# A resting rule for background chains, and a hand-laid start of the last attention

## The chip, the cores and the metric

The kernel runs on one core of one Trainium2 chip. Its time is the device time of one execution in microseconds (us), the median over several executions. All data are fp32. The core has a matrix engine (PE, with its weight loads shown apart as PEld), a vector engine (DVE), an activation engine (ACT), a general engine (POOL) and a sync engine (SP) that issues most of the DMAs. Each engine works through its own instructions strictly in the order in which the program lists them, and waits in place where an instruction's inputs are not there yet.

## The reference

Four layers, each an attention-like block and a feed-forward block, both with a residual connection and a layer norm before and after. x is 8 batches of 512 rows of 128 numbers.

```python
x = x + ln(attn0(ln(x)))     # softmax attention, 16 heads of 8; norm of its output over a whole batch
x = x + ln(mix(ln(x)))       # two mixes with the row before, sigmoid gate, squared relu
x = x + ln(learn(ln(x)))     # a scan: batch b's gradient step gives the weights for batch b and later ones
x = x + ln(switch(ln(x)))    # each row to one of 8 experts, half capacity, in order of rows
x = x + ln(linear_attn(ln(x)))
x = x + ln(experts(ln(x)))   # 8 experts choose 512 rows each, results are scatter-added
x = x + ln(rope_attn(ln(x))) # softmax attention with rotary positions, 16 heads of 8
x = x + ln(ffn4(ln(x)))      # 4 dense experts, 128 to 512 to 128, weighted per row

def ln(x):
    m = jnp.mean(x, axis=-1, keepdims=True)
    v = jnp.var(x, axis=-1, keepdims=True)
    return (x - m) / jnp.sqrt(v + 1e-5)
```

The scan in learn and the order of rows in switch make batches follow one another; everything else is independent from batch to batch up to the experts, which need all rows.

## The kernel before

A batch of x lies in SBUF as 128 partitions by 4 blocks (NJ = 4) by 128. The program is written with Python generators: there is no scheduler behind it, so the order in which the generators are advanced is the order of instructions on every engine.

**First attention.** `Attention.run` loops over g. There are 32 calls (8 batches, 4 groups of 4 heads), and a call has 4 values of g. In one g it issues 4 score matmuls (at_s, L410), each followed by a maximum on DVE (at_mx, L411), and, 7 values of g later for the same data, 4 transposed score matmuls (at_st, L417), each followed by an exponential on ACT (at_e, L420). Once in 4 values of g, `bg.rest()` runs, then the weighted sums of a whole call (at_o, 16 matmuls, L428), then `bg.pull`, then `taken`, which copies at_o out of PSUM on ACT (at_ot, L439). In the other three values of g only `bg.pull` runs. PSUM is used as a ring of 8 banks: score k+8 needs the bank of score k, so PE cannot run ahead of DVE and ACT by more than one g. With a bank for at_o the same holds.

**Background.** Beside the attention, `Background` advances generators ("chains"): `project` (norm, projections and stores for the next batch), `residuals`, `Mix.chain`, `Learn.prepare`, `Learn.chain`, `Learn.serve_chain` and `Route.chain`. A piece of a chain is what lies between two yields. Each yield gives an estimate of PE and DVE time, and `free(...)` marks a piece that may also be taken in `rest`. `pull` gives each chain one turn, until the estimates reach their bounds; `rest` makes two passes over the chains that are marked free, until the DVE estimate reaches 6. A gap below means what `rest` and the `pull` behind it do at one g, or a `pull` alone.

**A norm in a chain.** `norm_pieces` (L221) does: statistics on DVE (`stats`, L203 to L188) and the power on POOL (L194); yield free; a second yield free (`soft`, left out when `cx.brisk`); the offset on DVE (L211) and four scalings on ACT (L217); yield free; a `soft` yield. Up to three steps of a chain can thus fall into one gap with `rest`, so that the offset can stand on DVE right behind the power that it needs, and the scalings on ACT ahead of at_ot. `residuals` waits six turns after a batch's attention results were stored before it adds them.

**Rounds.** When the loop is over, `cx.brisk` is set and `Rounds.turn` advances what is left of the chains, and the new chains `Passes` (the switch layer's experts, in two passes: after 5 batches are routed and after 8) and `Pairs` (linear attention and the scores of the experts), one step each per round. Then `Experts.run` gathers, computes and scatter-adds (L1710).

**Last attention.** `l3` runs the same loop with `Background(3.3, 2.5)`, where `beside` is None and `rest` does nothing; the last layer's feed-forward is its background. Before the loop can start, `project(0)` must be done: `Experts.residual` loads four partial sums of batch 0 (L1749, four DMAs of 256 KB on SP), adds them (DVE for batch 0, POOL for others, L1754), norms the sum, adds it to x (POOL, L1758); then x is normed, turned (L239), copied (L240) and multiplied (L1790), and the rotary step goes over DVE and POOL (L1792 to L1801). `fill` (L376) then issues four loads of q and k (L381) and one of zeros (L382) on SP.

Of the kernel before, what the change touches and what calls it, by code (L numbers as in the profile page):

```python
# [17 lines left out]
P = 128  # L18
B = 8
S = 512  # L20
# [50 lines left out]
class Ctx:  # L71


    def __init__(self, es: ExitStack, tc: tile.TileContext, consts: bass.AP):
# [23 lines left out]
        self.brisk = False  # L98

# [121 lines left out]
    def norm_pieces(self, dst, src, last=0.0):  # L221

        mv, rs = self.stats(src)
        yield free(0.0, 1.5)
        yield from self.soft(free())
        self.affine(dst, src, rs, self.offset(mv, rs))
        yield free()
        yield from self.soft(last)
# [18 lines left out]

def costs(c):

    return (*c, False)[:3] if isinstance(c, tuple) else (c or 0.0, 0.0, False)  # L250


class Background:
# [14 lines left out]

    def add(self, gen):
        self.first.append(gen)  # L270
# [4 lines left out]
    def step(self, queue, gen):  # L275
        try:
            pe, dve, is_free = costs(next(gen))
        except StopIteration:
            queue.remove(gen)
            return  # L280
        self.pe += pe
        self.dve += dve
        (self.free.add if is_free else self.free.discard)(gen)

# [6 lines left out]
    def rest(self):  # L291

        if self.beside is None:
            return
        for _ in range(2):
            for gen in list(self.first):
                if self.dve >= self.beside:
                    return
                if gen in self.free:
                    self.turn(gen)  # L300
# [10 lines left out]
    def pull(self, spent=0.0):  # L311
# [4 lines left out]
        for gen in list(self.first):  # L316
            if self.pe >= max(pe - spent, 1.0) or self.dve >= dve:
                break
            self.turn(gen)
# [18 lines left out]
class Attention:  # L338
# [37 lines left out]
    def fill(self, n, sources, v):  # L376
# [3 lines left out]
        for h, src in enumerate(sources):  # L380
            nc.sync.dma_start(t[32 * h : 32 * h + 8], src)  # L381
# [104 lines left out]
def l0(cx: Ctx, at: Attention, Wq, Wk, Wv, mix, learn):  # L486
# [86 lines left out]
    def residuals():  # L573
        for b in range(B):
            while b not in finished:
                yield free()
            for _ in range(1 if cx.brisk else 6):
                yield free()
# [3 lines left out]
    def residual(b):  # L582
        y, xn = ys.pop(b), xns.pop(b)
        nc.gpsimd.tensor_add(y, y, xn)
        yield from cx.soft(free())
# [22 lines left out]
        yield free(0.2)  # L608
# [5 lines left out]
        yield free()  # L614
# [16 lines left out]
class Mix:  # L631
# [41 lines left out]
    def batch(self, b):  # L673
# [40 lines left out]
        yield free()  # L714


class Learn:
# [219 lines left out]
    def serve(self, b, xt, weights):  # L937
# [25 lines left out]
        yield free()  # L963
# [476 lines left out]
class Experts:  # L1440
# [303 lines left out]
    def residual(self, cx, b):  # L1744
# [7 lines left out]
        adds = nc.gpsimd if b else nc.vector  # L1752
        for i, k in ((0, 1), (2, 3), (0, 2)):
            adds.tensor_add(parts[:, i], parts[:, i], parts[:, k])  # L1754
# [14 lines left out]
def l3(cx: Ctx, at: Attention, experts, ffn, weights):  # L1769
# [8 lines left out]

    def project(b):
        yield from experts.residual(cx, b)  # L1780
        xn = cx.work([P, NJ, D], "xn")
        yield from cx.norm_pieces(xn, cx.x[b])
        xt = cx.work([P, S], "xnT")
        cx.flip(xt, xn)
        yield 0.5
# [196 lines left out]
def kernel(ctx: ExitStack, tc: tile.TileContext, a: dict, out: bass.AP):  # L1982
# [7 lines left out]
    with cx.phase("first"):  # L1990
# [6 lines left out]
        cx.brisk = True  # L1997
# [88 lines left out]
```

## Time and profile before

| what | value |
|---|---|
| three timed runs, us | 2119.72, 2121.99, 2127.91; median 2121.99 |
| profiled execution, its own time and its span, us | 2127.56 and 2125.8 |
| busy share of the span | PE 82%, DVE 60%, ACT 51%, POOL 24% |
| mean granted PE clock | 0.874 |
| first attention, first at_s to last at_o | 41.2 to 716.9 us |
| rounds, experts, to the last scatter L1710 | to 1299.8 us |
| start of the last attention, to its first at_s | to 1336.9 us |
| last attention and the end of the feed-forward | to 2125.8 us |

The span runs from the first to the last instruction; the profiled execution's own time is 1.8 us more. A sum of durations from the trace is compared with this execution, 5.6 us above the median of the timed runs. Busy PE counts matmuls in flight, so a PE that shows 95% is not at its peak.

### The profile page before, as it was taken

The page shows a single profiled execution, that of the slowest core. Times are in us where ns is not written, and L with a number is a line of the kernel's source. Part 1 is how long each engine was busy: PE and PEld are TensorE (multiplying, and loading weights), DVE is VectorE, ACT ScalarE, POOL GpSimd, SP SyncE. Part 2 cuts the span into 40 slices and gives each one's busy share as a digit, 9 for nine tenths or more (in the row PEclk, how much of TensorE's full clock was granted, in tenths as well). Part 3 has the DMA queues.
Part 4 walks back from the last instruction along what each step waited for, and adds up shares of the span by engine and source line. Part 5 has one row for each costly group of instructions (what it writes and reads, how often), then busy time and mean ns, then how long its engine had stood idle before and what let it go on. Part 6 is the DMA issues. An engine that isn't in the chain of part 4 may idle for free.

```text
span 2125.8 us, 31834 instructions
## 1 busy us (share of the span) xinstructions
PE 1740.0 (82%) x10886; PEld 1001.3 (47%) x10886; DVE 1282.0 (60%) x4012; ACT 1086.6 (51%) x2272; POOL 501.3 (24%) x566
## 2 busy tenths in 40 slices
PE   3999888988988777658546783799999999999996
PEld 1444344444434366547335562434554454545554
DVE  2777778767777546456447322777666666665522
ACT  1667656555554523256551221366666565565653
POOL 1001111212120312352523385222112121110001
PEclk8999899989999769569565786799999999999998
DMA  5212102111000213025223132111101010100000
GB/s 129 40 34 37 34 14 39 26 28 33 21 21 12 59 35 106 21 65 150 74 65 110 23 43 38 31 32 29 25 10 32 12 27 11 29 12 6 9 6 10
DMA packets 198065, 81.84 MB, mean 38 GB/s; under 512 B 97604, under 2 KB 189674, under 8 KB 197904
## 3 DMA queue, kind: packets, MB, share of 16 engines
q1 hardware_dynamic: 190224, 73.61, 14.4%
q0 software_dynamic: 7680, 6.19, 1.9%
q8 instruction: 87, 1.43, 0.3%
q14 instruction: 74, 0.61, 0.1%
HBM read 45.25 MB, written 31.59 MB: 36 GB/s over the span
## 4 chain that ended last, share of the span: by engine, by line
PE 31%; DVE 10%; POOL 4%; issue 3%; ACT 3%; DMA 1%; SPq 0%; POOLq 0%; ACTq 0%; DVEq 0%
PE at_s L410 6%; PE l3f_y_ps L1954 5%; PE at_o L428 5%; PE l3f_h_ps L1947 5%; DVE at_mx L411 4%; PE at_st L417 3%; POOL l2f_out L1710 2%; PE flip L239 1%; POOL l2f_xg L1105 1%; DVE ln_st L203 1%; PE l_qkv_ps L1790 1%; DVE l2f_junk L1530 1%; DMA l2f_xg<-l2f_x,l2f_idx 1%; DVE l_u L1799 1%; POOL ln_rs L194 1%
## 5 line engine op out<-in xcount | busy, mean ns | idle before, releaser
L411 DVE TENSOR_REDUCE at_mx<-at_s 128x1 f32<-128x512 f32 x1024 | 637.3, 682 | 287.2 <-PE at_st L417 219.6
L420 ACT ACTIVATE at_e<-at_st 128x512 f32<-128x512 f32 x1024 | 536.6, 600 | 197.4 <-PE at_st L417 170.7
L410 PE MATMUL at_s<-qk 32*128 32x512 f32 x2048 | 591.5, 655 | 44.6 <-DMA qk<-qk_zero 20.7
L417 PE MATMUL at_st<-qk 32*128 32x512 f32 x2048 | 582.5, 644 | 8.8 <-ACT at_ot L439 5.5
L410 PEld LDWEIGHTS at_s<-qk 32*128 32x128 f32 x2048 | 229.1, 194 | 196.0 <-DVE at_mx L411 62.8
L194 POOL TENSOR_TENSOR ln_rs<-ln_ve,mhalf 128x4 f32<-128x4 f32 x136 | 138.4, 1018 | 767.8 <-DVE ln_ve L188 701.7
L428 PE MATMUL at_o<-at_e,pad_v 128*32 128x512 f32 x2048 | 252.2, 636 | 35.4 <-DVE at_mx L411 35.4
L417 PEld LDWEIGHTS at_st<-qk 32*128 32x128 f32 x2048 | 229.7, 189 | 84.4 <-issue 47.0
L428 PEld LDWEIGHTS at_o<-at_e,pad_v 128*32 128x32 f32 x2048 | 67.2, 116 | 213.0 <-issue 178.8
L1954 PEld LDWEIGHTS l3f_y_ps<-w3f,l3f_hT 128*128 128x128 f32 x1024 | 131.2, 196 | 46.5 <-issue 27.8
L1954 PE MATMUL l3f_y_ps<-w3f,l3f_hT 128*128 128x128 f32 x1024 | 136.4, 281 | 3.3 <-ACT l3f_hT L1948 2.0
L1947 PE MATMUL l3f_h_ps<-l3f_xT,w3f 128*128 128x512 f32 x256 | 130.1, 607 | 0.0
L1948 ACT ACTIVATE l3f_hT<-l3f_h_ps,w3f_b1c 128x512 f32<-128x512 f32 x128 | 85.0, 683 | 63.0 <-PE l3f_h_ps L1947 63.0
L1957 DVE SCALAR_TENSOR_TENSOR l3f_o<-l3f_y_ps,l3f_w,l3f_o 128x128 f32<-128x128 f32 x128 | 43.9, 348 | 92.2 <-PE l3f_y_ps L1954 92.2
L217 ACT ACTIVATE l_xn<-x,ln_off,ln_rs 128x128 f32<-128x128 f32 x96 | 39.5, 482 | 88.5 <-DVE ln_off L211 82.7
L439 ACT COPY at_ot<-at_o 128x512 f32<-128x512 f32 x64 | 37.3, 583 | 73.2 <-PE at_o L428 73.2
L239 PE MATMUL flip<-consts_sb,l_xn 128*128 128x128 f32 x96 | 28.3, 389 | 53.4 <-ACT l_xn L217 53.1
L1091 POOL DMA_INDIRECT l1f_taken<-l1f_xn,l1f_place x32 | 33.1, 1035 | 119.5 <-issue 35.7
L203 DVE BATCH_NORM_STATS2 ln_st<-x 128x6 f32<-128x128 f32 x256 | 55.2, 278 | 9.1 <-POOL x L1397 3.3
L383 POOL COPY pad_v<-l_in 128x128 f32<-128x128 f32 x32 | 9.5, 297 | 202.3 <-DMA l_in<-l_v 160.8
L1710 POOL DMA_INDIRECT l2f_out<-l2f_y,l2f_idx x32 | 50.5, 1579 | 25.7 <-DVE l2f_y L1707 16.8
L1947 PEld LDWEIGHTS l3f_h_ps<-l3f_xT,w3f 128*128 128x128 f32 x256 | 42.2, 194 | 23.0 <-issue 9.6
(412 smaller groups left out, 2547.7 us busy)
## 6 DMA issues: line engine op xcount, KB each, us to landing
l1f_w<-in_L_ffn_w SPq DMA_DIRECT2D x32, 256.0 KB
l2f_parts<-l2f_out SPq DMA_DIRECT2D x32, 256.0 KB
l2f_out<-l1f_zero SPq DMA_DIRECT2D x24, 256.0 KB
l_qk<-l_qkT SPq DMA_DIRECT2D x16, 256.0 KB
qk<-l_qk SPq DMA_DIRECT2D x128, 32.0 KB
qk<-at_mt SPq DMA_DIRECT2D x256, 2.0 KB
qk<-l_qkT SPq DMA_DIRECT2D x128, 32.0 KB
l2f_x<-l2f_rows SPq DMA_DIRECT2D x8, 272.0 KB
```

The lines of the kernel that those rows point to most:

```text
L194: self.nc.gpsimd.tensor_tensor(rs, ve, self.mhalf[:, :NJ], ALU.pow)
L203: nc.vector.bn_stats(st[:, j, :], src[:, j, :])
L239: self.nc.tensor.transpose(t[:, j * P : (j + 1) * P], src[:, j, :], self.ident)
L410: nc.tensor.matmul(s, qk[:, 0, c * P : (c + 1) * P], qk[:, 1, :], start=True, stop=True)
L411: nc.vector.tensor_reduce(mx[n][:, c, h : h + 1], s, AX.X, ALU.max, negate=True)
L417: nc.tensor.matmul(s, qk[:, 1, c * P : (c + 1) * P], qk[:, 0, :], start=True, stop=True)
L420: nc.scalar.activation(es[g][:, h, :], s, AF.Exp, scale=scale)
L428: nc.tensor.matmul(o[32 * h : 32 * h + 32, :], vp[:, c, h, :], e[:, h, :], start=(c == 0), stop=(c == NJ - 1),)
L1710: nc.gpsimd.indirect_dma_start(out=self.pairs.summed[s], out_offset=bass.IndirectOffsetOnAxis(ap=idx[e][:, s : s + 1], axis=0), in_=ys[e][ ...
L1947: nc.tensor.matmul(hp, self.w1[:, e, f * P : (f + 1) * P], xt, start=True, stop=True)
L1948: nc.scalar.activation(hts[e][:, f], hp, AF.Relu, bias=self.b1c[:, f, e : e + 1])
L1954: nc.tensor.matmul(yp[:, :D], hts[e][:, f, js], self.w2[:, e, f, :], start=(f == 0), stop=(f == NF - 1))
```

## The change

Parts of the diff are left out where a line is only "...". The option `paced` is on in the first attention alone: it is set off together with `brisk` on and stays off.

```diff
@@ -97,6 +97,8 @@
 
         self.brisk = False
 
+        self.paced = True
+
     RING = 8
 
     @contextmanager
@@ -221,11 +223,16 @@
     def norm_pieces(self, dst, src, last=0.0):
 
         mv, rs = self.stats(src)
-        yield free(0.0, 1.5)
-        yield from self.soft(free())
+        yield later(free(0.0, 1.5))
+        yield from self.pause(free())
         self.affine(dst, src, rs, self.offset(mv, rs))
-        yield free()
-        yield from self.soft(last)
+        yield later(last if self.paced else free())
+        yield from self.pause(last)
+
+    def pause(self, cost=0.0):
+
+        if not self.paced:
+            yield from self.soft(cost)
 
     def soft(self, cost=0.0):
 
@@ -245,9 +252,16 @@
     return pe, dve, True
 
 
+def later(c=0.0):
+
+    return *costs(c)[:3], True
+
+
 def costs(c):
 
-    return (*c, False)[:3] if isinstance(c, tuple) else (c or 0.0, 0.0, False)
+
+    c = c if isinstance(c, tuple) else (c or 0.0, 0.0)
+    return (*c, False, False)[:4]
 
 
 class Background:
@@ -266,6 +280,8 @@
         self.bulk = []
         self.free = set()
 
+        self.asleep = set()
+
     def add(self, gen):
         self.first.append(gen)
 
@@ -274,13 +290,15 @@
 
     def step(self, queue, gen):
         try:
-            pe, dve, is_free = costs(next(gen))
+            pe, dve, is_free, waits = costs(next(gen))
         except StopIteration:
             queue.remove(gen)
             return
         self.pe += pe
         self.dve += dve
         (self.free.add if is_free else self.free.discard)(gen)
+        if waits and self.beside is not None:
+            self.asleep.add(gen)
 
     def turn(self, gen):
 
@@ -292,11 +310,11 @@
 
         if self.beside is None:
             return
-        for _ in range(2):
+        for _ in range(3):
             for gen in list(self.first):
                 if self.dve >= self.beside:
                     return
-                if gen in self.free:
+                if gen in self.free and gen not in self.asleep:
                     self.turn(gen)
 
     def between(self):
@@ -316,7 +334,9 @@
         for gen in list(self.first):
             if self.pe >= max(pe - spent, 1.0) or self.dve >= dve:
                 break
-            self.turn(gen)
+            if gen not in self.asleep:
+                self.turn(gen)
+        self.asleep.clear()
         while self.bulk and self.pe + spent < pe:
             self.step(self.bulk, self.bulk[0])
         self.dve = max(self.dve - dve, 0.0)
@@ -378,7 +398,9 @@
         nc = self.cx.nc
         t = self.qks[n % self.NQK]
         for h, src in enumerate(sources):
-            nc.sync.dma_start(t[32 * h : 32 * h + 8], src)
+
+            q = nc.scalar if n == 0 and h % 2 else nc.sync
+            q.dma_start(t[32 * h : 32 * h + 8], src)
         nc.sync.dma_start(t[8:P:32, 0, :], self.zero)
         nc.gpsimd.tensor_copy(self.pads[n % self.NPAD][:, :, :, 0:8], v)
 
@@ -574,15 +596,15 @@
         for b in range(B):
             while b not in finished:
                 yield free()
-            for _ in range(1 if cx.brisk else 6):
-                yield free()
+            for _ in range(1 if cx.brisk else 3 if cx.paced else 6):
+                yield later(free())
             yield from residual(b)
             mix.ready.append(b)
 
     def residual(b):
         y, xn = ys.pop(b), xns.pop(b)
         nc.gpsimd.tensor_add(y, y, xn)
-        yield from cx.soft(free())
+        yield from cx.soft(later(free()))
 
 
         st = cx.work([P, 6], "l0_st")
@@ -605,13 +627,13 @@
         nc.vector.tensor_scalar(ve, ps[:, 0:1], 1.0 / P, EPS, ALU.mult, ALU.add)
         rs = cx.work([P, 1], "l0_rs")
         nc.gpsimd.tensor_tensor(rs, ve, cx.mhalf[:, 0:1], ALU.pow)
-        yield free(0.2)
+        yield later(free(0.2))
         nc.vector.tensor_scalar(y, y, mean, rs, ALU.subtract, ALU.mult)
         yield from cx.soft(free(0.0, 0.7))
         t = cx.work([P, NJ, D], "l0_ln", bufs=1)
         yield from cx.norm_pieces(t, y, free())
         nc.gpsimd.tensor_add(cx.x[b], cx.x[b], t)
-        yield free()
+        yield later(free())
 
     projects[0] = project(0)
     bg.add(projects[0])
@@ -711,7 +733,7 @@
         t = cx.work([P, NJ, D], "l0f_t")
         yield from cx.norm_pieces(t, o, free())
         nc.gpsimd.tensor_add(cx.x[b], cx.x[b], t)
-        yield free()
+        yield later(free())
 
 
 class Learn:
@@ -960,7 +982,7 @@
         yield from cx.norm_pieces(t, o, free())
         nc.gpsimd.tensor_add(cx.x[b], cx.x[b], t)
         self.route.ready.append(b)
-        yield free()
+        yield later(free())
 
 
 class Route:
@@ -1749,9 +1771,8 @@
             nc.sync.dma_start(parts[:, i], self.by_tile(part, b))
         for _ in range(3):
             yield free()
-        adds = nc.gpsimd if b else nc.vector
         for i, k in ((0, 1), (2, 3), (0, 2)):
-            adds.tensor_add(parts[:, i], parts[:, i], parts[:, k])
+            nc.gpsimd.tensor_add(parts[:, i], parts[:, i], parts[:, k])
             yield free()
         t = cx.work([P, NJ, D], "ln_out")
         yield from cx.norm_pieces(t, parts[:, 0], free())
@@ -1776,13 +1797,74 @@
     turned, vs, os, projects = {}, {}, {}, {}
     bg = Background(3.3, 2.5)
 
+    def start():
+
+        xn = cx.work([P, NJ, D], "xn")
+        xt = cx.work([P, S], "xnT")
+        parts = cx.work([P, 4, NJ, D], "l2f_parts", bufs=1)
+        t = cx.work([P, NJ, D], "ln_out")
+        x = cx.x[0]
+        n = NJ // 2
+        halves = [slice(0, n), slice(n, NJ)]
+        for js in halves:
+            for i, part in enumerate(experts.pairs.summed):
+                q = nc.scalar if i % 2 else nc.sync
+                q.dma_start(parts[:, i, js], experts.by_tile(part, 0)[:, js])
+
+        def moments(src):
+            st = cx.work([P, n, 6], "ln_st2")
+            mv = cx.work([P, n, 2], "ln_mv2", bufs=4)
+            for j in range(n):
+                nc.vector.bn_stats(st[:, j, :], src[:, j, :])
+            for j in range(n):
+                nc.vector.bn_aggr(mv[:, j, :], st[:, j, :])
+            ve = cx.work([P, n], "ln_ve2", bufs=4)
+            nc.vector.tensor_scalar_add(ve, mv[:, :, 1], EPS)
+            rs = cx.work([P, n], "ln_rs2", bufs=4)
+            nc.gpsimd.tensor_tensor(rs, ve, cx.mhalf[:, :n], ALU.pow)
+            return mv, rs
+
+        def scaled(dst, src, mv, rs):
+            off = cx.work([P, n], "ln_off2", bufs=4)
+            nc.vector.scalar_tensor_tensor(off, mv[:, :, 0], -1.0, rs, ALU.mult, ALU.mult)
+            for j in range(n):
+                one = slice(j, j + 1)
+                if j % 2:
+                    nc.vector.tensor_scalar(dst[:, j, :], src[:, j, :], rs[:, one], off[:, one], ALU.mult, ALU.add)
+                else:
+                    nc.scalar.activation(
+                        dst[:, j, :], src[:, j, :], AF.Identity, bias=off[:, one], scale=rs[:, one]
+                    )
+
+        found = []
+        for js in halves:
+            for i, k in ((0, 1), (2, 3), (0, 2)):
+                nc.vector.tensor_add(parts[:, i, js], parts[:, i, js], parts[:, k, js])
+            found.append(moments(parts[:, 0, js]))
+        for js, f in zip(halves, found):
+            scaled(t[:, js], parts[:, 0, js], *f)
+        found = []
+        for js in halves:
+            nc.vector.tensor_add(x[:, js], x[:, js], t[:, js])
+            found.append(moments(x[:, js]))
+        for js, f in zip(halves, found):
+            scaled(xn[:, js], x[:, js], *f)
+            ps = cx.bank("flip")
+            for j in range(n):
+                nc.tensor.transpose(ps[:, j * P : (j + 1) * P], xn[:, js][:, j, :], cx.ident)
+            nc.scalar.copy(xt[:, js.start * P : js.stop * P], ps[:, : n * P])
+        return xt
+
     def project(b):
-        yield from experts.residual(cx, b)
-        xn = cx.work([P, NJ, D], "xn")
-        yield from cx.norm_pieces(xn, cx.x[b])
-        xt = cx.work([P, S], "xnT")
-        cx.flip(xt, xn)
-        yield 0.5
+        if b == 0:
+            xt = start()
+        else:
+            yield from experts.residual(cx, b)
+            xn = cx.work([P, NJ, D], "xn")
+            yield from cx.norm_pieces(xn, cx.x[b])
+            xt = cx.work([P, S], "xnT")
+            cx.flip(xt, xn)
+            yield 0.5
         qk = cx.work([P, NJ, 2 * H, 8], "l3_qk", bufs=1)
         v = vs[b] = cx.work([P, NJ, D], "l3_v")
         for j in range(NJ):
@@ -1994,7 +2076,7 @@
             learn = Learn(cx, route, *of("L1_attn", "t_k", "t_v", "t_q", "W1", "b1", "W2", "b2"))
             chains = l0(cx, Attention(ca), *of("L0_attn", "Wq", "Wk", "Wv"), mix, learn)
 
-        cx.brisk = True
+        cx.brisk, cx.paced = True, False
         with cx.beside("between") as cb:
             rounds = Rounds(chains)
             passes = Passes(cb, route, *of("L1_ffn", "w1", "b1", "w2", "b2"))
```

What it does, part by part:

1. `later` makes a yield a waiting one. In `step`, when the background has a bound `beside` (first attention alone), a waiting yield puts the chain into `asleep`; neither `rest` nor the `pull` of the same gap advances a chain that sleeps, and the end of `pull` wakes all.
2. `rest` makes three passes instead of two.
3. With `paced`, `norm_pieces` has two waiting yields instead of four plain ones. The yields behind the additions to x, behind the POOL addition and the power of `residual`, and the turns that `residuals` waits are waiting ones too; it waits three turns instead of six.
4. `fill` issues two of the four q and k loads of call 0 on ACT's queue instead of SP's, in both attentions.
5. `project(0)` of the last attention runs the new `start`: the four partial sums come in two halves of two row blocks, 8 DMAs of 128 KB, alternately on SP and ACT; sums, statistics, powers, scalings, the addition to x (DVE instead of POOL) and the turns are issued stage by stage, both halves of a stage before the next stage; of the scalings half are on DVE and half on ACT.

## The prediction

> **What bounds the kernel now.** I read the page's busy shares and slices first, to see the stages; then the table of windows, one early and two late in the first attention and one in the last; then PE's waits in the first attention; then the chain that ended last at the start of the last attention.
>
> ```profile
> PE 1740.0 (82%) x10886; PEld 1001.3 (47%) x10886; DVE 1282.0 (60%) x4012; ACT 1086.6 (51%) x2272; POOL 501.3 (24%) x566
> PE   3999888988988777658546783799999999999996
> DVE  2777778767777546456447322777666666665522
> PEclk8999899989999769569565786799999999999998
> ```
>
> A slice is 53 us. PE is the busiest engine in both attentions (slices 2 to 13 and 26 to 40), and low in the rounds between. In the first attention it is fuller at its beginning than later, and the granted clock falls with it.
>
> ```profile
> core 0: us, PE busy (x) PEld busy (x) DVE busy (x) ACT busy (x) POOL busy (x), PEclk, DMA share, GB/s
> 100.00:150.00 50.00, 49.06 (x359) 22.76 (x355) 38.71 (x79) 34.58 (x67) 3.13 (x5) 1.00 0.25 42
> 450.00:500.00 50.00, 45.54 (x327) 24.35 (x323) 38.30 (x113) 26.33 (x57) 4.68 (x5) 0.91 0.10 23
> 500.00:550.00 50.00, 40.83 (x284) 19.25 (x277) 38.38 (x127) 31.67 (x72) 13.36 (x15) 0.94 0.19 36
> 1700.00:1750.00 50.00, 49.66 (x362) 27.36 (x358) 33.18 (x87) 32.66 (x66) 11.94 (x13) 1.00 0.12 28
> ```
>
> At 450 to 550 PE is idle for 13.6 us of 100; at 1700 for 0.3 of 50. The ten windows from 200 to 700 sum to 68 us of idle PE at a mean clock of 0.92. So the late first attention has slack that the last one has not. What PE waits for there:
>
> ```profile
> PE at_o L428 <- DVE at_mx L411: 33.4, 17, 3.8
> PE at_s L410 <- DVE at_mx L411: 9.6, 10, 3.7
> PE at_s L410 <- ACT at_ot L439: 7.6, 7, 2.1
> PE at_st L417 <- ACT at_ot L439: 5.5, 3, 2.7
> ```
>
> The columns are the total, the times and the longest wait. Two things to see: at_o waits for DVE, which is late with the maxima because background work stood among them in the gaps before; and the scores behind at_o wait for ACT's copy at_ot, which stands behind the scalings of norms.
>
> ```profile
> 1312.48 1.66 ACT ln_out L217 x4
> 1314.26 1.26 POOL x L1758
> 1321.08 1.66 PE l_qkv_ps L1790 x2
> 1332.29 0.69 SPq L381
> 1335.03 1.79 DMA qk<-qk_zero
> 1336.86 2.08 PE at_s L410 x5
> ```
>
> This is the chain into the last attention: each line a start and a length. It is serial, so a microsecond saved there is saved at the end.
>
> **The change, part by part.** Parts 1 to 3 reorder the first attention and the rounds. I compared the instruction order of the two programs on each engine and priced each background instruction at its line's median duration in the trace.
>
> (a) *Work moved into the loop.* The chains run ahead. Counted in calls of 16 score matmuls, batch 3's routing comes at 31.0 before and at 29.0 after, batch 4's after the loop before and just inside it after; batch 5's update of learn comes behind the loop in both, in round 4 before and in round 1 after. Background DVE work in the loop goes from 177.3 to 185.7 us: 8.4 more; its matmuls are one batch's transposes, gradients and one routing. What a microsecond costs there: in the timeline the first nine at_o blocks start 15.3 us apart (75.8 to 198.3), with 1.9 us of DVE background per call; from 329.2 to 688.1 fifteen steps take 23.9 each, with 7.9. (23.9 - 15.3)/(7.9 - 1.9) = 1.4 us per us, the other engines' share in it. So +12.
>
> (b) *DVE ahead of at_o.* The gap just before at_o's g holds 41.9 us of background DVE work before and 36.7 after, over calls 12 to 31; the gap before that 34.9 and 24.0. The work goes to the gap at at_o itself (46.4 to 60.0), where at_o keeps PE busy for 3.6 us, and to the one behind (28.8 to 37.8). The five waits of over 3 us (303.9, 449.3, 497.3, 639.5, 688.1) all follow gaps with 3.0 or 3.1 us of it; the five with 1.3 or 1.4 had none or 0.8. That is (3.5 - 0.3)/1.7 = 1.9 us of wait per us, and for 5.2 us less -10; the gap before may add as much as its 11 us or nothing. The larger burst at at_o takes some back. I take -7, from 0 to -20.
>
> (c) *ACT ahead of at_ot.* Between the last at_e and at_ot stood 84.7 us of ACT background over 32 calls, often two or three norms' scalings (5.0 to 6.3 us); now 35.6. The norms' offsets: in the loop 4 stood in the same gap as their statistics, 10 one gap later, 23 two or three; now 32 one gap later, 7 more, none in the same. The waits on at_ot are 7.6 + 5.5 = 13.1 us; by 35.6/84.7 they fall to 5.5: -7.6. Nothing of it was hidden, since the waits are PE's. I take -7, from -2 to -13.
>
> (d) *Clock.* A mean of 0.92 over 500 us loses at most 40 us of PE time. The drop follows idle: from 397.4 to 404.2 PE is busy for 4.87 of 6.80 us at 0.99, and from 404.3 to 411.1 the clock is 0.51. If idle falls from 68 to 54, 14/68 of 40 is 8, of which I count half, as DVE is as late as PE: -4, from 0 to -10. The Trainium skill (TensorE: Matmul & The Clock Gate, Part 1) has the clock fall after an idle window of about 3.4 us; here it fell with no gap of over 1.7 us in the 6.8, so the trace disagrees, and by that rule this term would be near nothing.
>
> Sum of the first attention: 12 - 7 - 7 - 4 = -6.
>
> (e) *The rounds.* Both programs have 92 rounds, and the chain of rounds from batch 7's residual is the same. Batch 5's update falls at 758.6, at_ops at 725.1: four rounds in 33.5 us, 8.4 each; the 38 from there to the end of the last routing, 943.6, take 4.9 each. With the update gone from rounds 1 to 4 they would take 4.9: -14. But batch 7's result must go to memory and back, l_mean starts only at 739.6, and the first pass moves into the emptied rounds. I take -9, from -2 to -16.
>
> (f) *Start of the last attention.* Before: SP issues 1301.9, first sum 1307.17, first qkv 1321.08. After, from the same rows: 8 DMAs on two queues at 0.72 each, the first half issued by 1303.4, all by 1304.8 as before. A load took 3.4 to 3.8 us from issue to the sum that waited for it, the small zeros 1.8: the first half is there between 1305.2 and 1307.2, I take 1306. On ACT's queue only scalings that need these loads stand behind them. Half a sum is 0.35, three 1.1; statistics 0.44 + 0.18 + 0.17; power 1.0. The second half's sums and statistics (1.9) cover the first's power: both powers done at 1311.2. Offset, scaling and addition of the first half: 1312.1; both halves' statistics to 1314.1; second power 1315.2; the first half's flip and copy 1316.2. So -4.9 (1321.08 before). Then fill: the zeros go third and not fifth on SP's queue, 2 x 0.65 = -1.3. Together -6.2, from -3 to -8. What can go against it: the two-input sums run beside POOL. l_u (L1800) takes 279 ns alone and 758 ns beside POOL's product. Four such meetings would be 1.9 us. The Trainium skill (SBUF — State Buffer, "SBUF: two separate sides") says that a DVE operation with two SBUF inputs and a POOL operation that reads SBUF lock one another out; the trace agrees with 758 against 279 ns. By it the sum would be -4.3.
>
> (g) *Start of the first attention.* The same two loads on ACT's queue: qk loads at 37.73, zeros at 39.09, 0.33 each: -0.6. ACT has nothing to do until 51.9 there, so its wait costs nothing.
>
> The instructions of the last attention behind the start are the same on PE and DVE in the same order, so nothing changes there; the experts neither. Sum: -6 - 9 - 6.2 - 0.6 = -21.8. Against the profiled execution's own 2127.6 that is 2105.8; this execution is 5.6 above the median of the timed runs, so against the median 2100.
>
> **Rivals.** *Even exchange*: PE's waits keep their sum (b, c, d nothing), since DVE's work is only shifted by a gap. Then +12 - 9 - 6.8 = -4: 2118. For it: DVE is busy 38 of 50 us in every window. Against: at_ot's 13 us are ACT's, and ACT's queue is the one emptied most. *Slower*: the burst at at_o decides. A gap there now holds up to 6.4 us of DVE work (4.9 before). Where it is above at_o's 3.6, the maxima of the next g come late by the rest: 9.5 us in seven gaps of calls 12 to 31, 4.8 in four before. If each of the seven also costs a clock window of 3.4 us at half, 1.7: +4.7 + 12. With nothing saved in (b) to (d), +12, the rounds at -6 and the start at -5: +18, 2140. It decides if the sum ahead of at_o doesn't matter to PE. Against: that at_o's waits followed the gap before it in each of the five. *All waits end*: (b) to (d) at their far ends, -43 + 12, the rounds -12, the start -6.8: -50, 2072. *The change does not act*: excluded for the order, which differs; for time it is the even exchange.
>
> **How the numbers follow.** Forecast 2100 with 0.57 (own range 2085 to 2112), even exchange 0.22, slower 0.09, all waits end 0.12. The range takes the forecast, the even exchange and the upper part of the fast case, and leaves out the slower one and the far end: 2075 to 2124. Within 0.5% means 2111.4 to 2132.6, about what a measurement of this kernel can tell from none. Faster by more: forecast and fast case, 0.69; with the low side of the even exchange 0.70. Slower by more: 0.08, nearly all of the slower rival. Within: 0.22.
>
> **What would show it.** (a, b, c) In the windows from 200 to 700: idle PE at about 54 us, clock 0.93 or more; waits of at_o on at_mx near 26 us, on at_ot near 6; at_o's last block at 706 to 714 instead of 716.9. (e) l_mean of batch 7 as long after at_ops as before (14.5 us), but the first pass's transposes (768.7) some 20 us earlier, the second pass's start (about 950) 14 to 18 earlier in all. (f) First l_qkv_ps 16 to 17 us after the last scatter's end (1299.8) and not 21.3; first at_s 31 after it, not 37. Wrong would be: at_o's waits as long as before, with at_s behind at_o now waiting for at_mx; or a loop that ends later than 720, by (a) alone.

## The result, and the profile after

The changed kernel takes 2114.40 us, the median of eleven runs (2104.85 to 2119.98); the kernel before, beside it on the same chip, 2122.98 (2119.72 to 2128.10). The ratio is 0.9955, with a 95% interval of 0.9939 to 0.9970. That is 8.6 us faster, where 21.8 were forecast.

The profiled execution of the changed kernel took 2104.85 us, its own lowest and 10 under its median, so a single stage of it is read together with that of other executions of the same order (a table below). First the page: busy time by engine, and PE, DVE and the granted clock in slices of 53 us.

```profile
PE 1725.3 (82%) x10886; PEld 995.5 (47%) x10886; DVE 1291.4 (61%) x4025; ACT 1084.6 (52%) x2269; POOL 502.4 (24%) x567
PE   3999888887988967658446774899999999999997
DVE  2777787777787665446447323777766666665521
PEclk7999999997989978659555786799999999999998
```

The work is the same. The rounds are over sooner, but in slices 8 to 14 PE is no fuller than it was. The windows of the same two stretches as before, and 200 to 700 us as one:

```profile
core 0: us, PE busy (x) PEld busy (x) DVE busy (x) ACT busy (x) POOL busy (x), PEclk, DMA share, GB/s
450.00:500.00 50.00, 41.14 (x306) 23.06 (x300) 36.56 (x99) 22.52 (x47) 8.97 (x10) 0.90 0.08 19
500.00:550.00 50.00, 41.24 (x244) 19.84 (x243) 34.71 (x127) 28.54 (x63) 11.36 (x14) 0.83 0.18 35
200.00:700.00 500.00, 431.12 (x2989) 225.81 (x2981) 387.96 (x1155) 288.69 (x618) 92.06 (x106) 0.93 0.13 25
```

Idle PE is 17.6 us of 100 in the first two rows (13.6 before) and 68.9 over the 500 (68 before). The forecast was 54. PE's waits from 50 to 730 us (total, times, longest):

```profile
PE at_o L450 <- DVE at_mx L433: 20.9, 13, 4.7
PE l1q_hT_ps L877 <- DVE l1q_c L870: 19.7, 5, 6.8
PE at_st L439 <- ACT l_qkT L543: 8.3, 3, 3.9
PE l_mean_ps L616 <- DVE at_mx L433: 5.1, 5, 1.5
PE l_var_ps L625 <- DVE at_mx L433: 5.0, 5, 1.0
...
PE at_s L432 <- ACT at_ot L461: 1.1, 1, 1.1
```

The two waits that the change was expected to shorten did get short: at_o behind the maxima from 33.4 to 20.9, the scores behind at_ot from 13.1 to 1.1 (the last row is all that is left of it), and at_ops, behind at_ot too, from 7.1 to 0.7. But the second row is new and as large as what the two gave. It is five waits, one for each batch that learn serves in the loop (serve is the chain that applies learn's weights to a batch; step is the one that makes the gradient step): PE stands for up to 6.8 us before it can turn (transpose) `l1q_c`, the end of serve's gelu, which DVE is still computing. One of them in the timeline (start, length, engine and line, what):

```profile
383.98 3.64 PE L450 MATMUL at_o<-at_e,pad_v 128*32 128x512 f32 x32
...
386.80 0.22 DVE L854 TENSOR_SCALAR l1q_c<-l1q_a 128x128 f32<-128x128 f32 x1
...
393.98 0.29 DVE L870 TENSOR_TENSOR l1q_c<-l1q_a,l1q_p 128x128 f32<-128x128 f32 x1
394.42 1.01 PE L877 MATMUL l1q_hT_ps<-consts_sb,l1q_c 128*32 128x128 f32 x4 [6.80 <-DVE l1q_c L870]
...
397.47 2.56 DVE L433 TENSOR_REDUCE at_mx<-at_s 128x1 f32<-128x512 f32 x4 [3.20 <-PE at_st L439]
```

The gelu has three pieces (L854 to L870, 7.5 us of DVE here). At this g `rest`, with its three passes, took all of them, and the `pull` behind at_o took the chain's next piece, the transposes (L877), in the same gap. PE is in order: with the transposes waiting, the scores of the next g wait behind them. So first PE stands 6.80 us for DVE, and then DVE, done with the gelu, stands 3.20 us for scores that could have been there. The order of instructions shows how often it happens. For the five batches, the g (counted from the first) in which the gelu begins, ends, and is turned:

```
kernel       begins/ends/turned                                     waits at the turn, us (times)
before       63/64/64  80/80/81  95/96/96  112/112/113  127/128/128   1.2 (2)
wait6        63/64/64  79/80/80  96/96/96  111/112/112  127/128/128  10.1 (4)
after        59/60/60  76/76/76  92/92/92  107/108/108  123/124/124  19.7 (5)
gelu_step    60/60/60  76/76/76  92/92/92  108/108/108  124/124/124  33.4 (5)
gelu_serve   59/60/61  76/76/77  92/92/93  108/108/109  124/124/125   none listed
```

All three in one gap: in none of five before, in one of five in wait6, in two of five after (the waits of 6.80 and 6.57 us), in all five in gelu_step. The other rows are of kernels that are told of below.

The stages, for the kernels whose order in the first attention is the old one, the changed one, or a variant of it that is run below. Each row is one profiled execution, so a row is worth some us; "loop" is from the first at_s to the start of the last call's at_o in the first attention, "routing" from the last at_ops to the end of the last routing, "start" from the end of the last scatter to the first at_s of the last attention, "idle" what PE was idle from 200 us to the last at_o, "clock" the granted clock from 200 to 690.

| kernel | loop | routing | start | last attention | idle PE | clock |
|---|---|---|---|---|---|---|
| before | 675.7 | 218.6 | 37.0 | 788.9 | 70.9 | 0.917 |
| before_again | 675.4 | 218.8 | 36.6 | 788.7 | 73.1 | 0.920 |
| start_alone (old order in the loop) | 677.7 | 215.1 | 32.2 | 787.3 | 71.8 | 0.921 |
| after | 686.3 | 200.6 | 32.3 | 787.1 | 70.9 | 0.934 |
| after_again | 697.2 | 200.2 | 32.6 | 789.8 | 71.3 | 0.915 |
| pace_alone (changed order in the loop) | 691.1 | 200.0 | 36.6 | 788.8 | 72.9 | 0.927 |
| two_passes | 683.0 | 203.4 | 32.0 | 787.4 | 66.9 | 0.931 |
| one_pass | 681.8 | 205.8 | 32.3 | 790.5 | 47.1 | 0.913 |
| wait6 | 674.0 | 226.8 | 32.3 | 790.5 | 61.0 | 0.920 |
| early3 | 707.4 | 202.4 | 37.1 | 788.3 | 80.7 | 0.923 |
| gelu_waits | 681.3 | 192.7 | 32.8 | 789.6 | 67.5 | 0.930 |
| gelu_serve | 680.1 | 192.8 | 32.8 | 787.0 | 68.1 | 0.934 |
| gelu_step | 716.1 | 189.7 | 31.3 | 788.4 | 86.8 | 0.913 |
| gelu_one | 675.1 | 205.0 | 32.3 | 787.2 | 60.2 | 0.909 |

Means of the first three rows against the next three: loop 676.3 and 691.5, +15; routing 217.5 and 200.3, -17. The start goes from 36.7 (the first two rows and pace_alone's) to 32.3 (the three rows among these six that have the new one), -4.4; the first at_s of the kernel comes 1.3 us earlier, and linear attention (186.3 to 184.7 in the mean) 1.5 shorter. Together some -9, which is the measured -8.6. The loop's +15 rests on profiles that spread over 11 us, but the medians ask for it too: without it the other terms would make the kernel 24 us faster.

The chain into the last attention (start, length, what), which answers to the one shown before:

```profile
1286.16 3.90 DMA l2f_parts<-l2f_out
1290.39 0.43 DVE l2f_parts L1842
...
1294.37 0.71 POOL ln_rs L1824
...
1299.93 0.40 ACT xn L1835
1300.37 0.69 PE flip L1854 x2
1301.06 1.29 PE l_qkv_ps L1872 x2
...
1313.33 2.45 DMA qk<-qk_zero
1315.91 2.05 PE at_s L432 x5
```

The last scatter ended at 1283.66; the first qkv follows it by 17.2 us (21.3 before), the first at_s by 32.3 (37.0 before).

### The profile page after: what moved, and what is told of

It is laid out like the page before. It is cut to its first block, busy times and chain, and to the rows that moved or that the text cites. A ratio compares the mean times of both kernels' runs of the same rounds, so it can differ in the third digit from the quotient of the medians.

```text
span 2103.0 us, 31831 instructions
## 1 busy us (share of the span) xinstructions
PE 1725.3 (82%) x10886; PEld 995.5 (47%) x10886; DVE 1291.4 (61%) x4025; ACT 1084.6 (52%) x2269; POOL 502.4 (24%) x567
## 5 line engine op out<-in xcount | busy, mean ns | idle before, releaser
L450 PE MATMUL at_o<-at_e,pad_v 128*32 128x512 f32 x2048 | 243.0, 616 | 23.0 <-DVE at_mx L433 23.0
L2039 DVE SCALAR_TENSOR_TENSOR l3f_o<-l3f_y_ps,l3f_w,l3f_o 128x128 f32<-128x128 f32 x128 | 43.8, 348 | 89.6 <-PE l3f_y_ps L2036 89.5
L219 ACT ACTIVATE l_xn<-x,ln_off,ln_rs 128x128 f32<-128x128 f32 x96 | 39.5, 482 | 79.1 <-DVE ln_off L213 79.1
L461 ACT COPY at_ot<-at_o 128x512 f32<-128x512 f32 x64 | 37.4, 584 | 71.8 <-PE at_o L450 71.8
L205 DVE BATCH_NORM_STATS2 ln_st<-x 128x6 f32<-128x128 f32 x252 | 54.2, 277 | 14.3 <-POOL x L983 12.2
L1879 POOL TENSOR_TENSOR l_qk<-l_r,consts_sb 128x256 f32<-128x256 f32 x32 | 22.0, 686 | 130.2 <-DVE l_r L1874 130.2
L1712 ACT ACTIVATE l2f_hT<-l2f_h_ps,w2f_b 128x512 f32<-128x512 f32 x32 | 22.0, 687 | 57.7 <-PE l2f_h_ps L1711 45.5
```

The costliest lines, as they stand in the source:

```text
L205: nc.vector.bn_stats(st[:, j, :], src[:, j, :])
L450: nc.tensor.matmul(o[32 * h : 32 * h + 32, :], vp[:, c, h, :], e[:, h, :], start=(c == 0), stop=(c == NJ - 1),)
```

## The experiments

**The parts alone.** Which of the two halves of the change brings the 8.6 us, and do they add up? The changed kernel was run again beside one with only the new start, and one with only the new order of the first attention and the rounds.

> The changed kernel once more, for a second profile and a tighter time. Expected 0.9955 of before (2113 to 2115 us). The first profile of it was of an execution at 2104.9 us, 10 us under its median, and that of before at 2127.6, 5 us over its median: so the stretch that differs from execution to execution should be seen. Theory: the first attention ends 9 us later than before in this profile too (last at_o at 725, before 717), and the stretch from there to the last scatter is what varies (554 us in the first profile, 575 before); here 560 to 568. Rival: the attention varies, and its last at_o falls at 717 to 720.

```diff
 # start_alone, against the changed kernel
-        self.paced = True
+        self.paced = False
...
-        if waits and self.beside is not None:
-            self.asleep.add(gen)
...
-        for _ in range(3):
+        for _ in range(2):
```

> Only parts 4 and 5: the two queues of fill and the new start of the last attention; the chains as before. Theory: the start gives -4.8 us as in the trace (37.0 to 32.3 us from the last scatter's end to the first at_s) and the first fill -0.6: ratio 0.9975 (0.9965 to 0.9985), more than half of the whole gain. Rival: the gain is lost again in the last attention's first calls, which catch up with the same DVE backlog: 0.9995 to 1.000.

For pace_alone, `fill` issues all its loads on SP again, and the last layer's `project(0)` goes through `experts.residual` with its sums on DVE, as before.

```diff
 # pace_alone, against the changed kernel
-            q = nc.scalar if n == 0 and h % 2 else nc.sync
-            q.dma_start(t[32 * h : 32 * h + 8], src)
+            nc.sync.dma_start(t[32 * h : 32 * h + 8], src)
...
-        if b == 0:
-            xt = start()
```

> Only parts 1 to 3, the resting rule; both starts as before. Theory: the first attention loses 8 us (last at_o 725), the rounds win 10 to 12: ratio 0.998 to 0.9985. Rival 1 (prediction): both win, 0.993. Rival 2: the rule loses what it wins, 1.000.

Measured, as ratios to the kernel before (median 2122.35): after_again 0.9951 (0.9936 to 0.9965), 2112.47 us; start_alone 0.9966 (0.9953 to 0.9980), 2115.45; pace_alone 0.9980 (0.9969 to 0.9990), 2117.97. In us -9.9, -6.9 and -4.4: they add up (-11.3) within the intervals, and the ratios are near those that were expected. The stages of after_again are not: the last at_o came at 736.7 and not at 725, and the stretch from the last at_ops to the last scatter, which was thought to vary, took 550 us (554 in the first profile). The start gives most of the gain; the resting rule with all its reordering gives 4.4, because it loses in the loop (691.1) nearly all that it wins in the routing (200.0).

**Passes in rest.** The transposes catch up with the gelu because `rest` takes up to three of its pieces in one gap. With two passes they come one gap later in four of the five batches, with one pass in all five.

```diff
 # two_passes; one_pass has range(1)
-        for _ in range(3):
+        for _ in range(2):
             for gen in list(self.first):
                 if self.dve >= self.beside:
```

> The changed kernel with two passes in rest instead of three. Theory: the third pass puts the whole gelu of serve and the transposes that need it into one gap at at_o, and PE stands there for DVE (l1q_hT_ps waits for l1q_c: 19.7 us in 5 waits in the first attention of the changed kernel, 1.2 before). With two passes the transposes come one value of g later in most batches: that wait falls under 5 us, the last at_o comes at 712 to 718 and the ratio is 0.988 to 0.992. Rival: the moved work itself (12 us) makes the loop longer; then the wait only moves and the ratio stays at 0.9955.

> The changed kernel with one pass in rest. The largest gap in the loop holds 3.9 us of DVE work (6.4 with three passes, 5.5 with two). Theory that the size of the burst in a gap is what costs: 0.988 to 0.992. Rival that only the transposes right behind their gelu cost: as two_passes, 0.992 to 0.994.

Two passes: 0.9928 (0.9911 to 0.9945), 2105.50 us; one pass: 0.9905 (0.9886 to 0.9924), 2101.25. Both are faster than the changed kernel, so the third pass costs. But the loop with two passes is 683.0, and not as short as expected (the last at_o at 722.7 and not at 712 to 718): the wait at L877 is down to 0.5 us, and others head the list.

```profile
PE at_mx_ps L411 <- DVE at_mx L433: 20.3, 4, 5.4
PE at_o L450 <- DVE at_mx L433: 19.3, 16, 4.7
```

The burst of DVE is still there, and PE meets it at the next thing that needs the maxima. In the traces the fullest gap keeps DVE busy with background for 8.1 us with two passes as with three, and for 5.4 with one; the prices of the instruction order had said 5.5, 6.4 and 3.9. One pass takes idle PE from 70.9 to 47.1 us, the aim of the forecast's terms (b) and (c), and yet the loop is 681.8, no better than with two; the clock there is 0.913, against 0.931 with two (last section).

**Moved work, or the resting rule?** In wait6, residuals wait six turns again, so that the loop holds as much background DVE work as before (177.8 us; 177.3 before, 185.7 after), under the new rule. In early3 the kernel before gets the shorter wait alone (187.5 us in the loop), under the old rule.

```diff
 # wait6, against the changed kernel
-            for _ in range(1 if cx.brisk else 3 if cx.paced else 6):
+            for _ in range(1 if cx.brisk else 6 if cx.paced else 6):
 # early3, against the kernel before
-            for _ in range(1 if cx.brisk else 6):
+            for _ in range(1 if cx.brisk else 3):
```

> The changed kernel with residuals waiting six turns again instead of three, the rest of the rule kept. By the instruction order the loop of the first attention then holds 177.8 us of DVE background work, as before (177.3), and not 185.7. Theory: the loop got longer mainly by the work moved into it, term (a): first at_s to last at_o falls from 686 to 697 us to 676 to 682, the stretch from there to the last routing grows back from 200 to 212 to 216, and the ratio stays near 0.9955. Rival: the packing of the gaps makes the loop longer, whatever its work: the loop stays at 688 or more, and the ratio is 0.999 to 1.003.

> The kernel before, residuals waiting three turns instead of six, nothing else: 187.5 us of DVE background work in the loop (177.3 before), with the old pieces, no resting. Theory, as for wait6: the loop grows by 10.2 times 1.4, to 686 to 692 us, the routing stretch falls from 218.6 to about 202, ratio 0.998 to 0.9995: the resting rule is not what wins the rounds. Rival: without the rule the earlier chains bring more waits, the loop is 695 or more, ratio over 1.000.

wait6: 0.9996 (0.9981 to 1.0012), 2121.24 us; early3: 1.0058 (1.0042 to 1.0074), 2134.10. Both missed what was expected. With the same work in the loop the new rule is worth next to nothing there: 674.0 against 676.3. Of its waits at_o is down to 17.7 us (33.4 before), but the one for the maxima at the scores is 13.8 (9.6 before) and the one at L877 10.1 (1.2 before).

```profile
PE at_o L450 <- DVE at_mx L433: 17.7, 10, 3.8
PE at_s L432 <- DVE at_mx L433: 13.8, 11, 3.7
PE l1q_hT_ps L877 <- DVE l1q_c L870: 10.1, 4, 5.5
```

The short routing does not come from the resting rule but from the moved work: early3 has it (202.4) under the old rule, wait6 has not (226.8, with 93 rounds instead of 92). The old rule carries the moved work worse: 10.2 us more DVE work made the loop 31 longer in early3; 8.4 us more made it 15 longer in the changed kernel. In early3 it is another product that stands right behind the DVE work it needs: `l_mean_ps`, in residuals, waits 13.1 us in five places for DVE's `l_mv` (none listed before), and the transposes only 1.6. So the resting rule is worth having with the earlier residuals, and not alone.

**The transposes behind the gelu.** The cause named above, tried by itself: the yield between gelu and transposes, which the change left as it was in both places, is made one that rests till the next gap.

```diff
 # gelu_waits, against the changed kernel; in step (L894) and in serve (L965)
-        yield 0.0, 0.6
+        yield later((0.0, 0.6))
```

> The changed kernel, three passes, with the yield between gelu and the transposes (in step and in serve) made a waiting one. The transposes then come one g after the gelu's last product in every batch. Theory: this is the part of two_passes that counts: l1q_hT_ps waits for l1q_c under 3 us, ratio 0.991 to 0.994. Rival: two passes win by the smaller burst; here the burst is as in the changed kernel apart from the transposes, and the ratio is 0.995 to 0.996.

gelu_waits: 0.9843 (0.9823 to 0.9862), 2090.23 us, better than expected and the fastest here. The kernel before was profiled once more for its stages, and the two places were tried one by one, and both with one pass.

> The kernel before once more, for a second profile of it. Its loop (first at_s to last at_o) should take 675 to 680 us (675.7 in the first profile, 677.7 in start_alone, whose loop has the same order), against 686 to 697 in three profiles of the changed order. If it takes 685 or more, the difference of the loops is within the spread between executions and the account by stages falls.

> Of gelu_waits only the half in serve: the waiting yield between gelu and the transposes of serve (l1q_hT). 91 rounds, as gelu_waits has, and not 92. Theory that PE's wait for l1q_c and the round less make up its gain: as gelu_waits, 0.983 to 0.987. Rival that step's half counts too: 0.988 to 0.992.

> Only the half in step (l1a_hT): also 91 rounds, but serve's transposes stay right behind their gelu, and the gap at at_o holds the most DVE work of all orders, 75.8 us over calls 12 to 31 (60.0 in the changed kernel). Theory: l1q_hT still waits some 20 us; only the round less is won: 0.990 to 0.994, with a loop as in the changed kernel. Rival that the full gap at at_o costs by itself: 0.995 or more.

> gelu_waits with one pass in rest: 92 rounds, the largest gap 4.7 us of DVE work (5.5), transposes one g after the last product. If the loop is what wins, as gelu_waits or better, 0.980 to 0.986; if the round less is what wins, 0.987 to 0.991.

before_again took 2122.92 us (one run), with a loop of 675.4, as expected. gelu_serve: 0.9866 (0.9846 to 0.9887), 2091.63 us, which can't be told from gelu_waits. gelu_step: 1.0034 (1.0023 to 1.0046), 2126.01, slower than both kernels, which was not expected. gelu_one: 0.9867 (0.9844 to 0.9890), 2092.95: nothing is added by one pass, whose shorter loop (675.1) goes with a longer routing (205.0, 92 rounds). PE's waits in gelu_step:

```profile
PE l1q_hT_ps L877 <- DVE l1q_c L870: 33.4, 5, 6.7
PE at_st L439 <- ACT l_qkT L543: 12.2, 4, 3.9
```

Resting in step alone moves learn's chain by a gap, and all five gelus of serve now begin, end and are turned in one gap, at 6.7 us each. The gaps at at_o hold 75.8 us of background DVE work in calls 12 to 31 (60.0 in the changed kernel, 46.4 before, all by the forecast's prices), and the loop grows from 691.5 to 716.1. This is what the rival on record said, that the full gap costs by itself, and the two can't be told apart here: DVE also waits 30.7 us for learn's products at `l1a_a` (13.2 in the changed kernel), and the loop grew by 25 us where the wait at L877 grew by 14. gelu_serve is the clean one. Only the yield in serve differs, the wait at L877 is gone, and the loop is 680.1, with as much work in it (in calls 12 to 31 the background keeps DVE busy for 162.6 us in its trace, 163.9 in the changed kernel's). The same gelu in gelu_serve's timeline:

```profile
383.81 3.64 PE L450 MATMUL at_o<-at_e,pad_v 128*32 128x512 f32 x32
...
386.63 0.22 DVE L854 TENSOR_SCALAR l1q_c<-l1q_a 128x128 f32<-128x128 f32 x1
...
393.59 0.29 DVE L870 TENSOR_TENSOR l1q_c<-l1q_a,l1q_p 128x128 f32<-128x128 f32 x1
393.80 2.48 DVE L433 TENSOR_REDUCE at_mx<-at_s 128x1 f32<-128x512 f32 x4
394.54 0.38 PE L411 MATMUL at_mx_ps<-consts_sb,at_mx 128*16 128x128 f32 x1 [5.15 <-DVE at_mx L433]
```

DVE's burst is as long as before, and PE still waits, 5.15 us; in the whole loop `at_mx_ps` now waits 20.6 us in four places, as much as the transposes did (19.7). But the scores of the next g were done first, so DVE goes from the gelu straight into the maxima (393.80), where it had stood for 3.20 us. They were also done at full clock: the clock is at half from 391.3 to 398.1 us in the changed kernel and from 391.8 to 398.7 here, so that a score matmul behind the wait takes 1.06 us there, and one ahead of it 0.59 here. DVE's largest wait from 200 to 700 us, in the changed kernel and in gelu_serve:

```profile
DVE at_mx L433 <- PE at_st L439: 47.6, 34, 6.1
DVE at_mx L433 <- PE at_st L439: 34.3, 35, 3.9
```

Both kinds of wait for scores together, DVE stands 39.5 us (54.4 in the changed kernel), though a part of that comes back at other pieces of learn: for `l1a_b` it waits 16.7 instead of 5.2. The idle time of PE alone (68.1 against 70.9) does not show the difference. Nor does this wait alone put the loops in order: it is 67.9 us before and 43.8 in gelu_step. A part of the 11 us may be the clock: it is 0.934 in gelu_serve and 0.915 to 0.934 in the three profiles of the changed order.

Of the 24 us between gelu_waits and the changed kernel, some 10 are the loop and 8 the routing: with 91 rounds to go and not 92 it takes 192.7 and not 200.3. The rest is within what one profile can tell. two_passes, which ends the same wait at L877 but keeps 92 rounds and a routing of 203.4, has the gain of the loop alone: 2105.5.

## Why the prediction came out as it did

The direction was right, and the likeliest case was not: 2100 was forecast, 2114.4 measured, inside the range of 2075 to 2124 and beyond the forecast's own range of 2085 to 2112. In the first attention the rival "even exchange" is what happened, and the end lies between the two because the rounds gave more than either had. That the direction came out is in part luck: with the forecast's own -9 for the rounds, a loop 15 us longer would have left a gain of about 1. The prediction's own sign of being wrong, a loop that ends later than 720, came (725.7 in the first profile, 736.7 in the second).

- **The sum of the first attention failed: -6 was forecast, about +15 came.** The step that failed is in (b) and (c): that a wait which ends is time saved. Each wait did fall, by more than was taken (at_o by 12.5 and at_ot by 12.0, where 7 was taken for each), and idle PE stayed where it was, 70.9 us. The forecast looked for the next late thing only in the maxima at at_s. The largest of them was the transposes behind the gelu, and the order of instructions shows it without a run: they stand in one g with the whole gelu in two of five batches, where before there was none. wait6, which has them without (a), shows what (b) to (d) are worth together: -2 by its profile (674.0 against 676.3), where -18 was taken.
- **(a) was undersized.** The moved work was priced at 1.4 us per us of DVE, +12. From wait6 to the changed order (the mean 691.5) the loop grows by 17.5 us for 7.9 us of DVE work, 2.2 per us. The price was a mean over the whole loop, while the moved pieces brought their matmuls to a place where they stand behind DVE (at L877 19.7 us, 10.1 in wait6); the yield in serve returns 11 of the 17.5.
- **(d) failed by itself.** Clock was to rise as idle fell. Idle did not fall, and where it did (one_pass), the clock did not rise. The 0.93 that was forecast stands in the first profile (0.934, with the idle time of before), and not in the second (0.915).
- **(e) was right in kind and undersized:** -9 taken, -17 came, just beyond its -2 to -16. It had two reasons to take less than the -14 of its sum, and neither held. Batch 7's l_mean was to come as long after at_ops as before; it came 9.1 us after it (14.5 before), 5 of the 17. And the first pass was to fill the emptied rounds. It did move there (its transposes came at 745.6, 768.7 before, though the loop ended 8.7 us later), but from that l_mean to the end of the last routing it is 191.5 us and not 204.0.
- **(f) was nearly right:** -6.2 taken; -4.8 came in the first pair of profiles, -4.4 in the means of the table. Two terms. The first qkv came 17.2 us after the last scatter's end and not 16.4. The stages up to the first half's flip and copy took what was forecast, 14.2 us from SP's first issue (1285.73 to 1299.93) and 14.3 in the sum: a sum took 0.42 and not 0.35, three of the four powers 0.70 to 0.80 and not 1.0. But the sum let qkv follow that copy, and `start` issues the second half's turn ahead of it: PE waits for the second half's xn (1299.83 to 1300.32 on ACT), turns it at 1300.37, and begins qkv at 1300.85, 0.9 us late. And the zeros landed in 2.45 us, where 1.79 was carried over; why is not shown. The Trainium skill (SBUF — State Buffer, "SBUF: two separate sides") has DVE operations with two SBUF inputs and POOL operations that read SBUF lock one another out, and the forecast's estimate with such a lock was -4.3. What came is near that, but not for that reason: no two-input sum of the start was stretched, all took 0.42 to 0.43 us.
- **(g)** was -0.6 and is -1.3, within what differs between two executions.
- The slower rival said that a burst at at_o would make the next maxima late. gelu_step, where all of it falls there, is slower than the kernel before, so such a burst can cost that much, together with the transposes behind it. In the changed kernel its share is not known apart from theirs, and the shorter routing covered both. Its price was low: by the traces the fullest gap holds 8.1 us of DVE background (6.2 before), and not 6.4 (4.9).

What stays open: how (b) and (c) and the bursts share the loop's time apart from learn's transposes, since idle PE is 67 to 73 us in five orders with loops from 675 to 697; how much of the 11 us that the yield in serve returns is clock; and why ACT's copy `l_qkT` became late (8.3 us in three waits, none shown before).

## What to carry to other kernels

When engines work in order and a hand-made order overlaps two streams, look past the wait that a change shortens: list for the new order every instruction of the bottleneck that stands in one gap with the end of a long chain on another engine, because it holds up all the independent work behind it. A rule "rest until the next gap" belongs ahead of the first instruction that makes the busiest engine wait, and not only ahead of slow engines' results; here one such yield (2091.6 us against 2114.4) was worth more than the rest of the change, some 8 of its 23 us by a round less. And count idle time on both sides of a ring: two orders with nearly the same idle PE differed by some 10 us in the loop, and the slower one is where DVE waited in turn for PE; that this is the whole reason is not shown.

## What the runs showed of the hardware

Two executions of one order in the loop (after and after_again) have loops of 686.3 and 697.2 us with the same idle PE (70.9 and 71.3); of the columns of the table the granted clock, 0.934 and 0.915, is what differs. A difference of 1 or 2% in a stage is not to be judged by one profile.

The clock can be at half while PE is never idle. From 303 to 317 us in one_pass, windows of 3.5 us:

```profile
303.00:306.50 3.50, 3.50 (x13) 2.47 (x12) 2.22 (x6) 1.51 (x3) 1.72 (x2) 0.54 0.18 36
306.50:310.00 3.50, 3.50 (x20) 3.06 (x24) 0.76 (x2) 0.85 (x3) 0.00 (x0) 0.50 0.04 7
310.00:313.50 3.50, 3.50 (x19) 1.54 (x15) 3.28 (x9) 2.84 (x7) 0.56 (x1) 0.50 0.11 28
313.50:317.00 3.50, 3.41 (x20) 0.80 (x20) 3.43 (x18) 2.05 (x4) 2.02 (x2) 0.51 0.06 17
```

PE is busy for 13.91 of 14 us at a clock of 0.50 to 0.54, and no wait of PE in that kernel's loop is longer than 2.6 us. A score matmul takes 1.06 us there, and 0.59 just before. The Trainium skill (TensorE: Matmul & The Clock Gate, Part 1) has the clock halved after an idle window of about 3.4 us and released after a busy one of the same length. These rows disagree in both: no such idle window came before (the longest idle stretch of PE from 282 to 303 us is 2.5), and the clock stayed down through these four busy ones. What does was not found here; less idle time alone does not.
